# A gated layer's first block: second projection as seven products, weight differences on VectorE, last norm on ScalarE

## The chip, the cores and the metric

The kernel runs on one core of one Trainium2 chip. A core has five engines that each work through their own queue in order: TensorE (PE in the profile; its weight loads are listed apart as PEld), VectorE (DVE), ScalarE (ACT), GpSimd (POOL) and SyncE (SP, which here only issues DMAs). The metric is the device time of one execution in microseconds; the median of three runs is given. Everything is float32.

## What is computed

A transformer block on x (2 batches of 1024 tokens, 256 wide) with a context of 154 tokens, 192 wide: self attention, cross attention, and a gated layer, each with a layer norm ahead and a residual behind it. The change touches the gated layer alone:

```python
h = _layernorm(x, ln3_g, ln3_b)
p = h @ ff_w1 + ff_b1
a, gate = (p[..., :D_FF], p[..., D_FF:])
h = a * jax.nn.gelu(gate, approximate=False) @ ff_w2 + ff_b2
return h + x
```

D_FF is 1024. The first projection is 256 to 2048 wide, the second 1024 to 256.

## The kernel before

Self attention and cross attention come first (loops over p and c in the code). Behind them runs the loop of this case, over 64 *half units* k. The 2048 tokens are cut into four blocks (`pair` 0 to 3) of 512 tokens; each block has eight *units* (n, one for each 128 of the 1024 inner columns f), and a unit has two half units: `gate_first` at even k, `gate_second` at odd k. So block 0 is k 0 to 15, block 1 k 16 to 31, and so on. The order of the instructions on every engine is the order in which the code writes them: nothing is reordered. An instruction that waits holds up all that is behind it on its engine.

**The first projection** is written as a fast 2x2 matrix product: seven products (numbers 1 to 7) of 256 columns take the place of eight, out of sums and differences of the two token halves and of weights. The names: `pa`, `pb`, `pc` are PSUM banks of the unit, `own` its four rows of 256 in SBUF. In `gate_first(n)` product 1 goes to `pa`, ScalarE copies it to `own` (L1056); then `gate_last(n-1)` does product 4 of the unit before, VectorE adds (L1088), GpSimd multiplies (L1090) and so finishes that unit's first token half in `ub`; then products 6 and 5 with an addition each on VectorE (L1060, L1062) that read the copy. In `gate_second(n)` product 2 is added into `pa` (over what L1056 has read), ScalarE does a Gelu (L1074); product 7 is added into `pb` (over what L1060 has read), VectorE adds (L1076); product 3 into `pc` (over what L1062 has read), VectorE adds (L1079), ScalarE does the second Gelu (L1080), GpSimd multiplies (L1081) and finishes the second token half.

**The second projection** of a block runs beside the next block's units: `sums` holds its pieces, and each half unit takes some from the list. For blocks 1 to 3 it is again a fast product: `partial(pair, i, m)` does group m of seven for token tile i, four products of 128 columns each, with weight differences `half["t"]` (made by `column_sums`, four instructions on GpSimd at half units 18 to 26) and row sums `half["s"]` (made by `row_sums`, four instructions on GpSimd for each two units). Group 1, 6, 3 and 7 are followed by additions to x on VectorE (L1170); after groups 3 and 7 a DMA on SP's queue stores a tile of 128 tokens. For block 0 it is the plain product: 32 products of 256 columns (L1200), two in each half unit from 16 on, four additions (L1210) and four stores. The differences and row sums lie in one tile `wx`, taken by `hold_sums` at half unit 16 from a pool with two buffers (tag pT), which also holds the turned probabilities of cross attention and the weights of the gated layer.

**The norm of the second batch** (`norm_beside("ff", B - 1)`) runs beside half units 7 to 19 in steps, one at each odd half unit: a step issues, in this order, the transposes of two tiles that were normalized a step ago (L280, TensorE, stored later on ScalarE, L295), the statistics of two new tiles (L240, L241, VectorE), the deviation of two (L246, L250, GpSimd), and the normalization of two (L256 on VectorE makes the offset, then two instructions on GpSimd, L267; on ScalarE, L270, in the norms that `narrow` names). The first normalization falls to half unit 11, the last to 17.

Other work beside the loop: the end of cross attention at half units 0 to 3 (`cross_values`), four pieces of its output projection at half units 4 to 6 (L467, added to x by L474 on VectorE), `token_sums` of the next block at half units 8, 24 and 40 (L1020 to L1023, four on GpSimd), and additions of the last bias (L320, GpSimd) at each third half unit from 13 on.

Of the kernel before, what the change touches and what calls it, by code (L numbers as in the profile page):

```python
# [8 lines left out]
F32 = mybir.dt.float32  # L9
AF = mybir.ActivationFunctionType  # L10
ALU = mybir.AluOpType
AX = mybir.AxisListType

P = 128
# [4 lines left out]
def tile_transformer_block(ctx: ExitStack, tc: tile.TileContext, a: dict, out: bass.AP):  # L19
    nc = tc.nc  # L20
# [3 lines left out]
    B, S, D = x.shape  # L24
# [7 lines left out]
    NT = S // P  # L32
    GT = 4
# [17 lines left out]
    NF = DF // P  # L51
    SH = GH // 2
    TF = 2
# [5 lines left out]
    wpool = ctx.enter_context(tc.tile_pool(name="w", bufs=1))  # L59
# [13 lines left out]
    def sum_tile(name):  # L73

        return ps_o.tile([P, HB], F32, tag="po", name=name)
# [22 lines left out]
    for n in names:  # L98
        k = n_of[n]
# [67 lines left out]
    for n in names[2:]:  # L167
        own = rows[row_of[n] - n_cols:row_of[n] - n_cols + n_of[n], :]
        p = HR if n in twice else P
# [51 lines left out]
    def norm_pieces(kind, b, first=False):  # L221

        ln = {"sa": "ln1", "ca": "ln2", "ff": "ln3"}[kind]
        g0, b0 = row_of[ln + "_g"], row_of[ln + "_b"]
        st = {}
        nh = NC if kind == "ff" else NH  # L230
        order = tile_order(kind)

        def stats(t):
            if t == 0:
                st["hT"] = hT[kind, b] = p2.tile(
                    [P, nh, NC * S // nh], F32, tag="hT", name=f"hT_{ln}_{b}")
            if t % 2 == 0:
                st["mv", t] = small.tile([P, 2, 2], F32, tag="mv", name=f"mv_{ln}_{b}_{t}")
            s6 = small.tile([P, 6], F32, tag="st", name=f"st_{ln}_{b}_{t}")
            nc.vector.bn_stats(s6, xt[b, order[t] // GT][:, order[t] % GT, :])  # L240
            nc.vector.bn_aggr(st["mv", t // 2 * 2][:, t % 2, :], s6)  # L241

        def deviation(t):
            mv = st["mv", t]
            var = small.tile([P, 2], F32, tag="var", name=f"var_{ln}_{b}_{t}")
            (nc.vector if first else nc.gpsimd).tensor_scalar(  # L246
                var, mv[:, :, 1], EPS, 1.0, op0=ALU.add, op1=ALU.mult
            )
            rstd = small.tile([P, 2], F32, tag="rstd", name=f"rstd_{ln}_{b}_{t}")
            nc.gpsimd.tensor_tensor(rstd, var, power, ALU.pow)  # L250
            st["rstd", t] = rstd

        def normalize(t):
            rstd = st["rstd", t]
            off = small.tile([P, 2], F32, tag="off", name=f"off_{ln}_{b}_{t}")
            nc.vector.scalar_tensor_tensor(  # L256
                off, st["mv", t][:, :, 0], -1.0, rstd, op0=ALU.mult, op1=ALU.mult
            )
            pool, tag = (one, "xn") if narrow(kind, b) and not first else (pp_, "P")

            xn = pool.tile([P, nh, 2, D // nh], F32, tag=tag, name=f"xn_{ln}_{b}_{t}")
            st["xn", t] = xn
            for i in range(2):
                xs = xt[b, order[t + i] // GT][:, order[t + i] % GT, :]
                xs, own = xs.rearrange("p (c d) -> p c d", c=nh), xn[:, :, i, :]
                if not narrow(kind, b) or first and i == 1:
                    nc.gpsimd.tensor_scalar(  # L267
                        own, xs, rstd[:, i:i + 1], off[:, i:i + 1], op0=ALU.mult, op1=ALU.add)
                else:
                    nc.scalar.activation(  # L270
                        own, xs, AF.Identity, bias=off[:, i:i + 1], scale=rstd[:, i:i + 1])

        def turn(t):

            n = 2 if first else 1
            bank = mm_tile if first and t == 2 else spare["bank"]
            ph = [bank(f"ph_{ln}_{b}_{t}_{i}") for i in range(n)]
            for i in range(2 * D // P):

                nc.tensor.transpose(  # L280
                    ph[i * n * P // (2 * D)][:, i % (2 * D // P // n) * P:][:, :P],
                    st["xn", t].rearrange("p c i d -> p (c i d)")[:, i * P:(i + 1) * P], ident)

            def store():
                k = NC * 2 * P // nh
                for c in range(nh):
                    own = st["hT"][:, c, t // 2 * k:(t // 2 + 1) * k]
                    turned = ph[c * n // nh][:, c % (nh // n) * k:][:, :k]
                    gain, shift = cols[:, g0 + c:g0 + c + 1], cols[:, b0 + c:b0 + c + 1]
                    if spare["turned"] or first and c < nh // 2:  # L290
                        nc.vector.tensor_scalar(
                            own, turned, gain, shift, op0=ALU.mult, op1=ALU.add
                        )
                    else:
                        nc.scalar.activation(own, turned, AF.Identity, bias=shift, scale=gain)  # L295

            return store

        return (
            [lambda t=t: stats(t) for t in range(NT)],  # L300
            *([lambda t=t, f=f: f(t) for t in range(0, NT, 2)] for f in (deviation, normalize, turn)),
        )

# [6 lines left out]
    def narrow(kind, b):  # L310

        return kind == "sa" or kind == "ca" and b < B - 1
# [649 lines left out]
    NPR = B * 2  # L962
# [120 lines left out]
    def gate_last(n):  # L1083

        pair, f = divmod(n, NF)
        pa, pb, pc, own = psum.pop(n)
        product(n, 4, pb, False)
        nc.vector.scalar_tensor_tensor(  # L1088
            own[:, 0, :], pb[:, :BT], biases(n)[0], own[:, 0, :], op0=ALU.add, op1=ALU.add)
        nc.gpsimd.tensor_tensor(ub[pair][0][:, f, :], own[:, 0, :], own[:, 3, :], ALU.mult)  # L1090
        if f == NF - 1:
            if pair:
                early, late = (1, 4, 2), (5, 6, 3, 7)
                if pair == NPR - 1:
                    sums.extend((pair, i, m) for m in early for i in range(TF))
                    sums.extend((pair, i, m) for i in range(TF) for m in late)
                else:
                    sums.extend((pair, i, m) for i in range(TF) for m in early + late)
            else:
                sums.extend((pair, i, e) for i in range(2 * TF) for e in range(NF))  # L1100

    sums, summed = [], {}

# [2 lines left out]
    def hold_sums():  # L1106

        wx = pt_.tile([P, 2 * NK, QH // 2], F32, tag="pT", name="wx").rearrange("p a b -> p (a b)")
        n1, n2 = NF // 2 * P, NF // 2 * BT
        half["t"] = {  # L1110
            i: wx[:, k * n1:(k + 1) * n1].rearrange("p (c d) -> p c d", d=P)
            for k, i in enumerate((5, 6, 7, 4))
        }
        half["s"] = [
            {
                i: wx[:, 4 * n1 + (3 * e + k) * n2:][:, :n2].rearrange("p (c t) -> p c t", t=BT)
                for k, i in enumerate((5, 6, 3))
            }
            for e in range(2)
        ]  # L1120
# [4 lines left out]
    def column_sums(n):  # L1125

        t = half["t"]
        nc.gpsimd.tensor_tensor(*[
            lambda: (t[5], quarter(0, 1), quarter(0, 0)),
            lambda: (t[6], quarter(1, 1), t[5]),  # L1130
            lambda: (t[4], quarter(1, 0), t[6]),
            lambda: (t[7], quarter(1, 1), quarter(0, 1)),
        ][n](), ALU.subtract)
# [56 lines left out]

    def sum_slot():

        pair, i, f = sums.pop(0)
        if pair:
            return partial(pair, i, f)
        if f == 0:
            summed[pair] = sum_tile(f"pf{pair}_{i}")
        own = summed[pair]
        j, e = divmod(i, TF)
        nc.tensor.matmul(  # L1200
            own[:, :D], lhsT=ub[pair][j][:, f, e * P:(e + 1) * P], rhs=w2[:, f, :],
            start=(f == 0), stop=(f == NF - 1),
        )
        if f < NF - 1:
            return None
        b, t = divmod(pair * 2 * TF + i, NT)

        def store():
            xs = xt[b, t // GT][:, t % GT, :]
            nc.vector.tensor_tensor(xs, own[:, :D], xs, ALU.add)  # L1210
            nc.sync.dma_start(out=out[b, t * P:(t + 1) * P, :], in_=xs)

        return store


    with tc.manual_schedule():
# [192 lines left out]
        for k in range(2 * FU):  # L1409
# [17 lines left out]
                out_pieces("ca", B - 1, NQ - 1, out_order("ca"))  # L1427
            if k % (2 * NF) == NF and k < 2 * FU - 2 * NF:
                token_sums(k // (2 * NF) + 1)
            for _ in range(min(2 if k < 4 * NF else 1, len(sums))):  # L1430
                run(sum_slot)
            flush(stores)
            run_work(0 if k <= len(CG) else 1 + k % 2, k % 2)
            if later and k > 12 and k % 3 == 1:
                later.pop(0)()
            if k == 2 * NF:
                hold_sums()
            if k in (2 * NF + 2, 2 * NF + 4, 2 * NF + 8, 2 * NF + 10):
                column_sums((k - 2 * NF) // 3)
            pair, at = divmod(k - 5, 2 * NF)  # L1440
            if pair > 0 and at % 4 == 0:
                row_sums(pair, at // 4)
        gate_last(FU - 1)
        row_sums(NPR - 1, NF // 2 - 1)
        while sums:
# [35 lines left out]
```

## Time and profile before

| | us |
|---|---|
| median of 3 runs | 1078.59 (1078.13 to 1078.92) |
| the profiled execution, its own time | 1078.65 |
| its span, first to last instruction | 1076.9 |
| block 0 of the gated layer (half units 0 to 15) | 910.2 to 947.2 |
| half units 16 to 31 | 947.2 to 986.0 |
| half units 32 to 63 | 986.0 to 1060.4 |
| what is left of block 3 | 1060.4 to 1076.9 |

How to read it: in the order of time a row gives the start and length in us, engine, line, operation, what is written and read, and in brackets how long the engine stood idle before and who released it. `x2` behind a row means that two instructions of that form follow each other. A product in float32 appears as two matmuls. The length of a matmul is modelled and longer than the step to the next one. In a group by line the two numbers behind the bar are the busy time of all and the mean in ns of one; in the answer to a single line the three numbers are the shortest, the median and the longest in ns.

### The profile page before, as it was taken

How to read it: one execution, taken by the hardware profiler on the slowest of the kernel's cores; microseconds unless marked ns; L12 is line 12 of the kernel's file. 1: busy time of each engine (PE TensorE's matmuls, PEld its weight loads, DVE VectorE, ACT ScalarE, POOL GpSimd, SP SyncE). 2: the span in 40 equal slices, each digit the busy share in tenths (PEclk: the TensorE clock that was granted, in tenths of full speed). 3: DMA queues.
4: the chain of work that ended last, by engine and by line, in shares of the span. 5: the costliest groups of instructions: out<-in, count | busy, mean ns of one | idle time of the engine just before them, and what ended most of it. 6: DMA issues, size and time to landing. Idle time of an engine off the chain costs nothing.

```text
span 1076.9 us, 45967 instructions
## 1 busy us (share of the span) xinstructions
PE 1065.6 (99%) x19060; PEld 712.3 (66%) x19060; DVE 875.2 (81%) x1283; ACT 651.0 (60%) x2081; POOL 765.4 (71%) x1600
## 2 busy tenths in 40 slices
PE   8999999999999999999999999999999999999998
PEld 6545657567565565566665655567766677788998
DVE  5789999998989989999989998978766777654554
ACT  5666767667666666666776666666566555242221
POOL 2677777778777787777777777768665687488774
PEclk9999999999999999999999999999999999999999
DMA  3232122111111111211211211135323221000000
GB/s 95 63 91 63 46 47 46 33 43 30 41 40 33 43 43 29 53 43 24 53 24 33 53 24 38 24 103 131 97 57 83 68 58 41 1 10 11 21 11 30
DMA packets 99234, 50.56 MB, mean 47 GB/s; under 512 B 30218, under 2 KB 97810, under 8 KB 99026
## 3 DMA queue, kind: packets, MB, share of 16 engines
q1 hardware_dynamic: 97698, 46.96, 18.0%
q8 instruction: 150, 2.46, 1.0%
q10 hardware_dynamic: 1328, 0.66, 0.2%
q14 instruction: 58, 0.48, 0.1%
HBM read 35.25 MB, written 3.41 MB: 36 GB/s over the span
## 4 chain that ended last, share of the span: by engine, by line
PE 91%; POOL 3%; DVE 2%; DMA 1%; ACT 1%; issue 1%; SPq 1%; DVEq 0%; POOLq 0%; ACTq 0%
PE s L493 19%; PE po L547 19%; PE py_sa L467 5%; PE py_ca L467 5%; PE pv_sa L393 5%; PE pq_ca L362 5%; PE pq_sa L362 5%; PE pk_sa L362 5%; PE sc L867 4%; PE poc L932 4%; PE pb L1037 3%; PE pf L1161 3%; PE pa L1037 2%; PE pc L1037 2%; PE pf L1200 1%; DMA st<-st 1%
## 5 line engine op out<-in xcount | busy, mean ns | idle before, releaser
L613 POOL TENSOR_SCALAR p<-p,rd,ee 128x512 f32<-128x512 f32 x508 | 387.4, 773 | 91.4 <-DVE rd L605 88.1
L508 ACT ACTIVATE p<-s,st 128x512 f32<-128x512 f32 x512 | 345.9, 687 | 175.5 <-DVE st L502 169.7
L502 DVE TENSOR_REDUCE st<-s 128x2 f32<-128x1024 f32 x256 | 308.8, 1207 | 51.1 <-issue 20.4
L640 DVE STREAM_TRANSPOSE pT<-p 128x1024 f32<-128x1024 f32 x256 | 302.4, 1219 | 1.5 <-POOL p L613 1.5
L493 PE MATMUL s<-k_sa,q_sa 64*32 64x512 f32 x4096 | 256.1, 591 | 2.4 <-ACT p L508 1.6
L547 PE MATMUL po<-pT,v_sa 64*32 64x256 f32 x8192 | 239.5, 376 | 0.9 <-ACT p L885 0.9
L547 PEld LDWEIGHTS po<-pT,v_sa 64*32 64x32 f32 x8192 | 177.5, 106 | 71.4 <-issue 26.2
L493 PEld LDWEIGHTS s<-k_sa,q_sa 64*32 64x32 f32 x4096 | 83.5, 106 | 101.0 <-issue 52.7
L885 ACT ACTIVATE p<-sc,neg 128x154 f32<-128x154 f32 x256 | 96.9, 401 | 74.9 <-DVE rden L893 74.4
L896 POOL TENSOR_SCALAR p<-p,rden 128x154 f32<-128x154 f32 x256 | 97.4, 402 | 61.7 <-DVE rden L893 61.2
L508 ACT ACTIVATION_READ_ACCUMULATOR p<-s,st 128x1 f32 x512 | 103.4, 202 | 0.0
L526 POOL TENSOR_TENSOR dd<-st 128x8 f32<-128x8 f32 x128 | 25.9, 202 | 73.5 <-DMA st<-st 69.7
L872 DVE TENSOR_REDUCE neg<-sc 128x6 f32<-128x924 f32 (+1 forms) x48 | 48.0, 1000 | 31.0 <-PE sc L867 30.9
L393 PEld LDWEIGHTS pv_sa<-sa_wv,hT_ln 64*128 64x128 f32 x1024 | 58.5, 188 | 14.2 <-issue 9.2
L393 PE MATMUL pv_sa<-sa_wv,hT_ln 64*128 64x128 f32 x1024 | 61.7, 275 | 0.0
L467 PE MATMUL py_ca<-ca_wo,o_ca 128*128 128x256 f32 x256 | 60.8, 385 | 0.0
L467 PE MATMUL py_sa<-sa_wo,o_sa 128*128 128x256 f32 x256 | 59.8, 386 | 0.0
L467 PEld LDWEIGHTS py_sa<-sa_wo,o_sa 128*128 128x128 f32 x256 | 47.2, 190 | 18.0 <-ACT v_sa L402 5.9
L362 PE MATMUL pq_ca<-hT_ln,ca_wq 64*128 64x512 f32 (+1 forms) x352 | 58.2, 589 | 0.0
L362 PE MATMUL pk_sa<-hT_ln,sa_wk 64*32 64x512 f32 x960 | 57.1, 590 | 0.0
L362 PE MATMUL pq_sa<-hT_ln,sa_wq 64*32 64x512 f32 (+1 forms) x976 | 56.7, 586 | 0.0
L885 ACT ACTIVATION_READ_ACCUMULATOR p<-sc,neg 128x1 f32 x256 | 55.3, 216 | 0.0
(132 smaller groups left out, 1442.6 us busy)
## 6 DMA issues: line engine op xcount, KB each, us to landing
v_sa<-v_sa SPq DMA_DIRECT2D x32, 256.0 KB, 3.8
st<-st SPq DMA_DIRECT2D x510, 1.0 KB, 1.8
v_ca<-vd SPq DMA_DIRECT2D x32, 160.0 KB, 3.1
sa_wq<-in_L_xattn_sa_wq_dram SPq DMA_DIRECT2D x32, 128.0 KB, 3.2
sa_wk<-in_L_xattn_sa_wk_dram SPq DMA_DIRECT2D x32, 128.0 KB, 3.2
sa_wv<-in_L_xattn_sa_wv_dram SPq DMA_DIRECT2D x32, 128.0 KB, 3.2
ca_wq<-in_L_xattn_ca_wq_dram SPq DMA_DIRECT2D x32, 128.0 KB, 3.4
wf<-in_L_xattn_ff_w_dram SPq DMA_DIRECT2D x12, 256.0 KB, 5.3
```

The lines of the kernel that those rows point to most:

```text
L362: nc.tensor.matmul(pq[r][f:f + m, at:at + n], lhsT=wt[own, c, f:f + m], rhs=h[own, c, t0:t0 + n], start=(c == 0), stop=(c == NH - 1), tile ...
L393: nc.tensor.matmul(pv[r][:, i * P:(i + 1) * P], lhsT=h[own, c, i * P:(i + 1) * P], rhs=wt[own, c, :], start=(c == 0), stop=(c == NH - 1), ...
L467: nc.tensor.matmul(py[:, e * D:(e + 1) * D], lhsT=o[:, i, (t + e) * P:(t + e + 1) * P], rhs=wo[kind, b, g][:, i, :], start=(i == 0), stop= ...
L493: nc.tensor.matmul(sc[a4 * KB:(a4 + 1) * KB, j, :], lhsT=q[r, c:c + KB], rhs=k[r, h * HB:(h + 1) * HB], start=True, stop=True, tile_positi ...
L502: nc.vector.tensor_reduce(st[:, 0, 0, i, :], sc, AX.X, ALU.max, negate=True)
L508: nc.scalar.activation(pr[:, j, :], sc[:, j, :], AF.Exp, bias=st[:, 0, 0, i, j:j + 1], accum_out=st[:, 0, 1, i, j:j + 1],)
L547: nc.tensor.matmul(po[a2][d:d + KB, :QH // 2], lhsT=v[r, t, e, d:d + KB], rhs=pT[r, d // DH * NK + n, :], start=(t == 0 and e == 0), stop= ...
L613: nc.gpsimd.tensor_scalar(pr[:, j, :], pr[:, j, :], v["rd"][:, c:c + 1], v["ee"][:, 0, c:c + 1], op0=ALU.mult, op1=ALU.mult,)
L640: nc.vector.transpose(halves[h][:, :, c:c + KB], slot[p]["members"][i].rearrange("p j (n k) -> p (j n) k", k=KB))
L885: nc.scalar.activation(pr_[:, j, i, :T], sc[:, j, i * T:(i + 1) * T], AF.Exp, bias=neg[:, j, i:i + 1], accum_out=den[:, j, i:i + 1],)
L896: nc.gpsimd.tensor_scalar(pr_[:, j, i, :T], pr_[:, j, i, :T], rden[:, j, i:i + 1], 1.0, op0=ALU.mult, op1=ALU.mult,)
L1037: nc.tensor.matmul(into[:, :BT], lhsT=lhs, rhs=wh[pair][i], start=first, stop=True, skip_group_check=True)
```

## The change

The second projection of block 0 goes through `partial` like the others: at the end of block 0 fourteen groups are put in `sums` (for each of two token tiles: 1, 4, 2, 5, 6, 3, 7), and one is taken in each half unit from 18 on (before: two plain products from 16 on). The plain path falls away. The row sums of block 0 are made at half units 6, 10, 14 and 17; those of blocks 1 to 3 move by up to two half units. `hold_sums` comes at half unit 4; the weight differences get four tiles of their own in the buffers of attention weights that are no longer used, and `column_sums` runs on VectorE, at half units 5 to 8. The normalization of the second batch's last norm runs on ScalarE.

```diff
@@ normalize
-                if not narrow(kind, b) or first and i == 1:
+                if not narrow(kind, b) and (kind, b) != ("ff", B - 1) or first and i == 1:
                     nc.gpsimd.tensor_scalar(
                         own, xs, rstd[:, i:i + 1], off[:, i:i + 1], op0=ALU.mult, op1=ALU.add)
                 else:
...
@@ gate_last
         if f == NF - 1:
-            if pair:
-                early, late = (1, 4, 2), (5, 6, 3, 7)
-                if pair == NPR - 1:
-                    sums.extend((pair, i, m) for m in early for i in range(TF))
-                    sums.extend((pair, i, m) for i in range(TF) for m in late)
-                else:
-                    sums.extend((pair, i, m) for i in range(TF) for m in early + late)
+            early, late = (1, 4, 2), (5, 6, 3, 7)
+            if pair == NPR - 1:
+                sums.extend((pair, i, m) for m in early for i in range(TF))
+                sums.extend((pair, i, m) for i in range(TF) for m in late)
             else:
-                sums.extend((pair, i, e) for i in range(2 * TF) for e in range(NF))
+                sums.extend((pair, i, m) for i in range(TF) for m in early + late)
@@ hold_sums
-        n1, n2 = NF // 2 * P, NF // 2 * BT
+        n2 = NF // 2 * BT
         half["t"] = {
-            i: wx[:, k * n1:(k + 1) * n1].rearrange("p (c d) -> p c d", d=P)
-            for k, i in enumerate((5, 6, 7, 4))
+            i: wpool.tile([P, NF // 2, P], F32, tag=tag, name=f"w2s{i}", bufs=2 if tag == "wq" else 1)
+            for i, tag in ((5, "wq"), (6, "wq"), (7, "wk"), (4, "wv"))
         }
...
@@ column_sums
-        nc.gpsimd.tensor_tensor(*[
+        nc.vector.tensor_tensor(*[
...
@@ sum_slot
-        pair, i, f = sums.pop(0)
-        if pair:
-            return partial(pair, i, f)
...
+        return partial(*sums.pop(0))
@@ the loop over half units
-            for _ in range(min(2 if k < 4 * NF else 1, len(sums))):
+            for _ in range(min(int(k > 2 * NF + 1), len(sums))):
                 run(sum_slot)
...
-            if k == 2 * NF:
+            if k == len(CG) + 1:
                 hold_sums()
-            if k in (2 * NF + 2, 2 * NF + 4, 2 * NF + 8, 2 * NF + 10):
-                column_sums((k - 2 * NF) // 3)
+            if len(CG) + 1 < k <= NF:
+                column_sums(k - len(CG) - 2)
+            if k in (NF - 2, NF + 2, 2 * NF - 2, 2 * NF + 1):
+                row_sums(0, (k - NF + 2) // 4 + k % 2)
             pair, at = divmod(k - 5, 2 * NF)
-            if pair > 0 and at % 4 == 0:
-                row_sums(pair, at // 4)
+            ready = (2, 4, 9, 12) if pair == 1 else (0, 3, 8, 12)
+            if pair > 0 and at in ready:
+                row_sums(pair, ready.index(at))
```

More of the change, by code (lines that the diff above doesn't have):

```diff
@@ L1115, in hold_sums @@
             {
-                i: wx[:, 4 * n1 + (3 * e + k) * n2:][:, :n2].rearrange("p (c t) -> p c t", t=BT)
+                i: wx[:, (3 * e + k) * n2:][:, :n2].rearrange("p (c t) -> p c t", t=BT)
                 for k, i in enumerate((5, 6, 3))
@@ L1191, in sum_slot @@
     def sum_slot():
-        pair, i, f = sums.pop(0)
-        if pair:
-            return partial(pair, i, f)
[L1196 to L1213, printed above, removed]
+        return partial(*sums.pop(0))
     with tc.manual_schedule():
```

## The prediction

> **What bounds the kernel now.** I read the page first (busy shares, chain of waits), then a table of stages over the gated layer, then the order of time of each engine between 930 and 957 us, where the edits fall.
>
> ```profile
> span 1076.9 us, 45967 instructions
> PE 1065.6 (99%) x19060; PEld 712.3 (66%) x19060; DVE 875.2 (81%) x1283; ACT 651.0 (60%) x2081; POOL 765.4 (71%) x1600
> PE 91%; POOL 3%; DVE 2%; DMA 1%; ACT 1%; issue 1%; SPq 1%; DVEq 0%; POOLq 0%; ACTq 0%
> ```
> ```profile
> 910.20:947.20 37.00, 35.66 (x237) 28.34 (x230) 26.23 (x71) 13.35 (x30) 18.74 (x32) 1.00 0.00 1
> 947.20:986.00 38.80, 38.80 (x187) 34.18 (x186) 19.35 (x46) 13.63 (x30) 34.59 (x49) 1.00 0.03 11
> 986.00:1021.40 35.40, 35.40 (x220) 32.67 (x219) 20.28 (x47) 10.39 (x23) 26.00 (x38) 1.00 0.05 16
> ```
> The columns are stretch, length, then busy time of TensorE, its weight loads, VectorE, ScalarE and GpSimd, clock, DMA. First row: half units 0 to 15 (gated units 0 to 7 of the first block); second: half units 16 to 31, where the old second projection of that block runs; third: what follows. TensorE has no idle time from 947.2 us on. Work taken from it there is worth its full length, and a wait put on it anywhere is lost. In the first row it is not full, and its order of time shows where:
>
> ```profile
> 933.90 0.59 PE L1037 MATMUL pa<-hT_ln,wf 128*128 128x256 f32 x2
> 934.63 0.70 PE L1037 MATMUL pb<-hT_ln,wf 128*128 128x256 f32 x2
> 937.32 0.59 PE L1037 MATMUL pa<-hT_ln,wf 128*128 128x256 f32 x2
> 938.05 0.70 PE L1037 MATMUL pb<-hT_ln,wf 128*128 128x256 f32 x2
> 940.75 0.59 PE L1037 MATMUL pa<-hT_ln,wf 128*128 128x256 f32 x2
> 941.84 0.70 PE L1037 MATMUL pb<-hT_ln,wf 128*128 128x256 f32 x2 [0.49 <-DVE own L1060]
> 942.80 0.27 PE L280 MATMUL ph_ln<-ident,xn_ln 128*128 128x128 f32 x1
> 943.24 0.55 PE L280 MATMUL ph_ln<-ident,xn_ln 128*128 128x128 f32 x3 [0.16 <-POOL xn_ln L267]
> 945.35 0.59 PE L1037 MATMUL pa<-hT_ln,wf 128*128 128x256 f32 x2
> 946.64 0.86 PE L280 MATMUL ph_ln<-ident,xn_ln 128*128 128x128 f32 x4
> 947.34 0.60 PE L1037 MATMUL pa<-hT_ln,wf 128*128 128x256 f32 x2
> ```
> One product of 256 columns is two matmuls and takes 0.43 us of TensorE (945.35 to 946.64 are three). Product 7 of units 4, 5 and 6 comes 0.73, 0.73 and 1.09 after product 2, so 0.30, 0.30 and 0.66 late; the transposes are 0.33 late (0.44 after the first where 0.11 is the step), and the second set, 0.44 long, is left after 0.70 and so costs another 0.26. In all 1.85 us wait, first on VectorE, then on GpSimd's norm. So half units 8 to 15 have no cover.
>
> **The change, part by part.**
>
> *The products.* Old: 32 products of 256 columns. New: 2 token tiles x 7 groups of 4 products of 128 columns.
>
> ```profile
> 985.51 0.86 PE pf L1200 x4
> 988.10 0.89 PE pf L1161 x8
> ```
> From the chain in order of time: two old products 0.86, one new group 0.89. Old 16 x 0.86 = 13.8 us (half units 16 to 31), new 14 x 0.89 = 12.5 us (18 to 31, one a half unit: just in time before the next block's groups at 32). Term: -1.3 us, full worth. The additions to the result grow on VectorE:
>
> ```profile
> L1170 DVE TENSOR_TENSOR x<-pf,x 128x512 f32<-128x512 f32 (+2 forms) x30 | 14.2, 478 | 16.0 <-PE pf L1161 15.8
> L1210 DVE TENSOR_TENSOR x<-pf,x 128x256 f32<-128x256 f32 x4 | 1.7, 425 | 2.0 <-PE pf L1200 2.0
> ```
> 10 of the first (4.8 us) replace 4 of the second (1.7): +3.1 us in a stretch where VectorE is busy 19.35 of 38.80. Nothing; without that cover at most 3.1. The output DMAs stay four on SP's queue, at half units 23, 24, 30, 31 instead of 19, 23, 27, 31: nothing, SP carries nothing else there. Memory of the weight differences: buffers of weights long used up, no instruction. The block's sums tile is taken at half unit 4, after its old content is read at 3: nothing.
>
> *Weight differences on VectorE, half units 5 to 8.*
>
> ```profile
> L1128 POOL TENSOR_TENSOR wx<-wf 128x512 f32<-128x512 f32 x2 | 2.5, 1273 | 0.0
> 925.89 0.69 DVE L474 TENSOR_TENSOR x<-py_ca,x 128x512 f32<-128x512 f32 x1 [1.30 <-PE py_ca L467]
> 927.62 0.69 DVE L474 TENSOR_TENSOR x<-py_ca,x 128x512 f32<-128x512 f32 x1 [1.03 <-PE py_ca L467]
> ```
> Leaving GpSimd frees 5.1 us at half units 18 to 26, where nothing waits for it. No two-SBUF-operand subtraction of 512 stands on VectorE; below it lies nothing, above it GpSimd's 1.27 plus one blocked turn of 0.73 (next fence but one); I take 0.62, a little under L474's 0.69 for as many elements, one operand of it in PSUM. The first two (half units 5, 6) fall into VectorE's waits for the output projection, 1.30 and 1.03 long here. The other two meet this:
>
> ```profile
> 932.37 0.42 DVE L1079 TENSOR_TENSOR own<-pc,own 128x256 f32<-128x256 f32 x1
> 933.42 0.72 POOL L1081 TENSOR_TENSOR kT<-own 128x256 f32<-128x256 f32 x1 [3.64 <-ACT own L1080]
> 933.79 0.45 DVE L1088 SCALAR_TENSOR_TENSOR own<-pb,cols,own 128x256 f32<-128x256 f32 x1
> 934.16 0.42 DVE L1060 TENSOR_TENSOR own<-pb,own 128x256 f32<-128x256 f32 x1
> 935.36 0.48 DVE L1076 SCALAR_TENSOR_TENSOR own<-pb,cols,own 128x256 f32<-128x256 f32 x1 [0.46 <-PE pb L1037]
> 937.59 0.41 DVE L1060 TENSOR_TENSOR own<-pb,own 128x256 f32<-128x256 f32 x1
> ```
> The third enters before L1088 at 933.79, waits for L1081 to end at 934.1, takes 0.62: L1060 slips 0.9, product 7 of unit 4 with it. The fourth enters before L1076, behind L1090: VectorE's gap of 0.46 takes part of it, 0.3 more remain. Product 7 of unit 5 is then 1.2 late.
>
> That two-operand work blocks across the engines is seen at 951.77:
>
> ```profile
> 951.77 0.73 POOL L320 TENSOR_TENSOR x<-x,ff_b 128x256 f32<-128x256 f32 x1
> 951.77 0.73 DVE L256 SCALAR_TENSOR_TENSOR off_ln<-mv_ln,rstd_ln 128x2 f32<-128x2 f32 x1
> L256 DVE SCALAR_TENSOR_TENSOR off_ln<-mv_ln,rstd_ln x24: 126/161/735, 6.6 to 951.8; 128x2 f32<-128x2 f32 x24
> ```
> Two numbers a partition usually take 0.16 us; here 0.73, exactly until L320 ends. [...]
>
> *Row sums of the first block, half units 6, 10, 14, 17.*
>
> ```profile
> L1140 POOL TENSOR_TENSOR wx<-u 128x256 f32<-128x256 f32 x12 | 8.7, 729 | 0.0
> 942.09 1.10 POOL L267 TENSOR_SCALAR xn_ln<-x,rstd_ln,off_ln 128x256 f32<-128x256 f32 x2
> ```
> Four such each: 2.9 us of GpSimd, 11.7 in all, against four norms of 1.10 taken off it. The first set falls into an idle 3.6 us (row 933.42). The others pile up: GpSimd is 4 to 6 us later at half unit 18. Its gate products feed nothing that is waited for soon, and group 5, which needs the last set (I get 957.3 to 960.3), runs after 963. But the norm's reciprocal deviations queue behind them.
>
> *Last norm on ScalarE, half units 11, 13, 15, 17.*
>
> ```profile
> L270 ACT ACTIVATE xn_ln<-x,off_ln,rstd_ln x20: 586/600/607, 6.8 to 612.9; 128x256 f32<-128x256 f32 x20
> 940.10 0.35 ACT L1056 COPY own<-pa 128x256 f32<-128x256 f32 x1
> 940.64 0.41 DVE L256 SCALAR_TENSOR_TENSOR off_ln<-mv_ln,rstd_ln 128x2 f32<-128x2 f32 x1
> 944.31 0.37 ACT L1056 COPY own<-pa 128x256 f32<-128x256 f32 x1 [0.33 <-PE pa L1037]
> 944.42 0.37 DVE L256 SCALAR_TENSOR_TENSOR off_ln<-mv_ln,rstd_ln 128x2 f32<-128x2 f32 x1
> ```
> Here the loss lies. ScalarE's queue gets two norms (1.1 us) that wait for L256, and behind them stands L1056, the copy of the next unit's product 1. Product 2 overwrites what that copy reads, and L1060 reads the copy; so TensorE and VectorE both stop until it is done. Today L1056 runs before L256 is over. Walking the queues: L256 at 941.7 (1.2 late, less a shorter block), norms to 943.0, L1056 to 943.3; product 2 of unit 6 starts 943.3 (today 940.75), product 7 943.8: 1.9 late. From there L1076, L1079 and two statistics give VectorE free at 946.7; the deviation needs GpSimd, which ends L1081 of unit 5 only after the second row sums, and gives it at 946.5; L256 gets its turn by 947.2, norms to 948.4, L1056 to 948.8; product 2 of unit 7 starts 948.8 against 945.35, product 7 3.6 late at 949.2 to 949.4. The third turn (no statistics left) costs 0.5, the fourth 0.3, where today's are the 0.26 of the transposes. From half unit 18 the groups between cover it. TensorE's waits: 1.25 and 0.6 at units 4 and 5, 1.5, 2.0, 0.5, 0.3 at units 6 to 9: 6.1, in place of 1.85 now: +4.2.
>
> **Sum.** -1.3 + 4.2 = +2.9 us on the span of 1076.9, that is 1079.8; that execution took 1078.65, 0.06 over the median, so the median goes from 1078.59 to about 1081.4. After half unit 32 nothing changes: the row sums of later blocks move by one or two half units beside a full TensorE, and the tail's own are where they were.
>
> **Bounds.** A difference at no cost leaves the norm's part: +1.6. At 1.3 a piece the two uncovered ones add 1.9: +4.8. Norms of 0.45 instead of 0.55 apart: 0.2 less. No row sums ahead of the deviations: 1 less.
>
> **The rivals.**
> 1. *Only the norm costs.* VectorE finds room for the differences, as for the first two. For it: its gap of 0.46 a unit. Against: no gap between 932.37 and 934.9. -1.3 + 2.9 = +1.6: 1080.2.
> 2. *The other side: ScalarE has room and TensorE stays the bound.* If the copies come out ahead of the norms, ScalarE, busy 13.35 of 37.00, takes them free, the transposes stop waiting for GpSimd (0.33 and 0.26) and the products' -1.3 counts: -1.9, 1076.7; with all of 1.85 gone 1075.4. It decides where L256 ends before a copy's product does, 0.5 us earlier than now. Against: L256 at 940.64, L1056 at 940.10.
> 3. *Blocking multiplies.* GpSimd's row sums and VectorE's differences and L256 shut each other out in turn, each difference takes 1.3, and the deviations come later: +4.8, 1083.4. For it: the 0.73. Against: L256 is held for one instruction only.
>
> **How the numbers follow.** Forecast 0.50, rival 1 0.20, rival 2 0.12, rival 3 0.18. About 0.2% (2.2 us) is what can be told from no change: slower means above 1080.75. The forecast with its own spread of 1080.2 to 1082.6 lies above in four fifths of its cases (0.40), rival 3 all (0.18), rival 1 a little (0.03): slower 0.61. Faster, below 1076.4, is half of rival 2: 0.06. Same 0.33. Range 1078.0 to 1083.8: it leaves out most of rival 2 and the top of rival 3.
>
> **What would show it.** In the changed profile: L1170 x40 and no L1200; TensorE full from half unit 18 on; L1056 of units 6 to 9 starting as the norm's second activation ends; product 2 waiting for ScalarE there, 4 us in all; VectorE's differences 0.6 to 0.7 when alone. Wrong if the copies run ahead of the norms, if product 7 of unit 5 is not about 1 us late, or if a group between half units 19 and 31 waits for GpSimd.

## The result, and the profile after

| | before | changed |
|---|---|---|
| median of 9 runs, us | 1078.46 (1077.61 to 1079.63) | 1081.41 (1080.77 to 1083.19) |
| profiled execution, its own time | 1078.65 | 1081.6 |
| its span | 1076.9 | 1079.8 |
| first product of half unit 0 to first product of half unit 32 ("the stretch") | 75.99 | 78.45 |

The changed kernel is slower: ratio 1.0029, 95% interval 1.002 to 1.0038. By the medians that is 2.95 us, by the interval between 2.2 and 4.1. The forecast was 1081.4.

The busy shares on the page of the changed kernel:

```profile
PE 1065.2 (99%) x19108; PEld 710.8 (66%) x19108; DVE 879.9 (81%) x1293; ACT 654.4 (61%) x2089; POOL 765.3 (71%) x1604
```

TensorE is busy 0.4 us less than before (1065.2 against 1065.6) and the span is 2.9 longer: what was added is waiting, not work.

Now the table of stages, laid from product to product so that both kernels are cut at the same instruction. First the kernel before, half units 0 to 15 and 16 to 31:

```profile
910.22:947.34 37.12, 35.78 (x238) 28.48 (x231) 26.37 (x71) 13.38 (x31) 18.88 (x32) 1.00 0.00 1
947.34:986.21 38.87, 38.87 (x186) 34.23 (x185) 19.21 (x45) 13.80 (x31) 34.66 (x49) 1.00 0.03 11
```

Then the changed kernel, the same two parts:

```profile
910.73:950.92 40.19, 35.80 (x239) 28.39 (x231) 28.91 (x74) 15.28 (x34) 24.49 (x38) 1.00 0.00 1
950.92:989.18 38.26, 38.13 (x234) 34.44 (x233) 21.77 (x52) 15.44 (x35) 31.59 (x47) 1.00 0.03 9
```

The stretch is 2.46 us longer with 0.7 less of TensorE's busy time in it. The loss lies in the first part, which is 3.07 longer: TensorE is idle 4.39 us there, 1.34 before. The second part is 0.61 shorter. It holds the products' gain of 1.3, and 0.7 of that is lost again in small delays at units 8 and 9. What follows the stretch is the same length in both (1076.9 - 986.21 = 90.7, 1079.8 - 989.18 = 90.6). The remaining 0.5 us of the span is older than the gated layer: its first product comes at 910.73 instead of 910.22, behind code that is the same in both. In the twelve traces of this study that first product falls between 909.41 and 912.29, so a single span can be off by a microsecond or two for reasons that have nothing to do with the edits. From here on kernels are compared by the stretch, and the medians stand beside it. The stretch is read from one execution of each kernel, but it repeats well: half units 0 to 7, which no edit lengthens, take 21.95 or 21.96 us in all twelve traces, and what follows half unit 32 takes 90.6 or 90.7.

The changed kernel's TensorE in order of time, each late product with the row ahead of it:

```profile
934.41 0.59 PE L1037 MATMUL pa<-hT_ln,wf 128*128 128x256 f32 x2
935.98 0.70 PE L1037 MATMUL pb<-hT_ln,wf 128*128 128x256 f32 x2 [0.98 <-DVE own L1060]
...
938.80 0.59 PE L1037 MATMUL pa<-hT_ln,wf 128*128 128x256 f32 x2
939.51 0.70 PE L1037 MATMUL pb<-hT_ln,wf 128*128 128x256 f32 x2
...
941.77 0.59 PE L1037 MATMUL pc<-hs,w1s 128*128 128x256 f32 x2
943.72 0.70 PE L1037 MATMUL pa<-hT_ln,wf 128*128 128x256 f32 x2 [1.35 <-ACT own L1056]
...
946.88 0.59 PE L1037 MATMUL pc<-hs,w1s 128*128 128x256 f32 x2
949.05 0.70 PE L1037 MATMUL pa<-hT_ln,wf 128*128 128x256 f32 x2 [1.58 <-ACT own L1056]
...
952.22 0.59 PE L1037 MATMUL pc<-hs,w1s 128*128 128x256 f32 x2
952.94 0.70 PE L1037 MATMUL pa<-hT_ln,wf 128*128 128x256 f32 x2
...
956.60 1.05 PE L1158 MATMUL pf<-wf,u 128*128 128x128 f32 x8
957.58 0.70 PE L1037 MATMUL pa<-hT_ln,wf 128*128 128x256 f32 x2
```

From each pair the step of 0.43 (0.89 behind the group of the last pair) is taken off. That leaves 1.14 at product 7 of unit 4, 0.28 at product 7 of unit 5, 1.52 at product 2 of unit 6, 1.74 at product 2 of unit 7, 0.29 at unit 8 and 0.09 at unit 9: 5.1 us, and with the lags of about 0.1 behind late products (0.53 or 0.54 to the next product, as from 935.98 to 936.52, instead of 0.43), as far as the kernel before doesn't have them too, some 5.6. The stretch says the same: 75.99 less the old waits of 1.85 less the products' 1.3 is 72.84, and 78.45 is 5.6 over that.

ScalarE of the changed kernel, in order of time, the two turns that cost most:

```profile
942.32 1.09 ACT L270 ACTIVATE xn_ln<-x,off_ln,rstd_ln 128x256 f32<-128x256 f32 x2 [0.68 <-DVE off_ln L256]
943.32 0.35 ACT L1056 COPY own<-pa 128x256 f32<-128x256 f32 x1
...
947.66 1.09 ACT L270 ACTIVATE xn_ln<-x,off_ln,rstd_ln 128x256 f32<-128x256 f32 x2 [1.34 <-DVE off_ln L256]
948.65 0.35 ACT L1056 COPY own<-pa 128x256 f32<-128x256 f32 x1
```

The copy that TensorE waits for starts in the moment the second normalization is over, and the normalizations start when L256 lets them: ScalarE itself had been idle for 0.68 and 1.34 us. Who holds L256 up is read from the chain of waits of the changed kernel, in order of time (start, length, engine, what):

```profile
942.14 0.69 POOL wx L1137
...
944.43 0.68 POOL kT L1140
945.12 0.69 POOL kT L1081
...
946.15 0.71 POOL rstd_ln L250
946.89 0.68 DVE off_ln L256
947.66 1.09 ACT xn_ln L270 x2
948.75 0.27 ACT own L1056
949.05 0.70 PE pa L1037 x2
```

The chain runs through GpSimd: the second set of row sums, then the multiply L1081, then the deviation L250, then VectorE's L256, and last ScalarE and TensorE. Two orders of issue thus lie on the path, row sums ahead of the deviation and norms ahead of the copy.

### The profile page after: what moved, and what is told of

Same layout as the page of the kernel before. It is cut to its first block, busy times and chain, and to the rows that moved or that the text cites. A ratio compares the mean times of both kernels' runs of the same rounds, so it can differ in the third digit from the quotient of the medians.

```text
span 1079.8 us, 46101 instructions
## 1 busy us (share of the span) xinstructions
PE 1065.2 (99%) x19108; PEld 710.8 (66%) x19108; DVE 879.9 (81%) x1293; ACT 654.4 (61%) x2089; POOL 765.3 (71%) x1604
## 4 chain that ended last, share of the span: by engine, by line
PE 88%; POOL 3%; DVE 3%; ACT 2%; DMA 2%; issue 1%; SPq 1%; DVEq 0%; POOLq 0%; ACTq 0%
PE s L493 19%; PE po L547 19%; PE py_sa L467 5%; PE py_ca L467 5%; PE pv_sa L393 5%; PE pq_sa L362 5%; PE pk_sa L362 5%; PE pq_ca L362 4%; PE pf L1158 4%; PE sc L867 4%; PE poc L932 4%; PE pb L1037 3%; PE pa L1037 2%; PE pc L1037 2%; DMA st<-st 1%; ACT p L508 1%
```

## The experiments

Theory: three edits put waits on TensorE in half units 8 to 17, where it has no cover. These are the third and fourth weight difference on VectorE, the norms ahead of the copy on ScalarE, and the row sums ahead of the deviations on GpSimd; only the order in the queues matters. The rivals are those of the prediction: the norm alone costs; the engines have room; blocking between VectorE and GpSimd is the main price. Ten kernels were run. Length of the stretch (by the table of stages, cut as above), median and ratio to the kernel before:

| kernel | stretch | against 75.99 | median, us | before, same chip | ratio, 95% interval |
|---|---|---|---|---|---|
| changed | 78.45 | +2.46 | 1081.41 | 1078.46 | 1.0029, 1.002 to 1.0038 |
| 1 changed, copies ahead of norms | 77.29 | +1.30 | 1080.29 | 1079.07 | 1.0014, 1.0004 to 1.0023 |
| 2 changed, differences early | 77.19 | +1.20 | 1081.04 | 1079.07 | 1.002, 1.001 to 1.0029 |
| 3 changed, row sums late | 77.80 | +1.81 | 1082.32 | 1079.07 | 1.0028, 1.0015 to 1.0041 |
| 4 changed, norm back on GpSimd | 82.40 | +6.41 | 1085.33 | 1079.07 | 1.0061, 1.0046 to 1.0076 |
| 5 before, norm on ScalarE | 77.98 | +1.99 | 1081.14 | 1079.12 | 1.0022, 1.0012 to 1.0031 |
| 6 before, norm on ScalarE behind the copy | 76.10 | +0.11 | 1079.44 | 1079.12 | 1.0003, 0.9994 to 1.0012 |
| 7 before, differences on VectorE | 77.07 | +1.08 | 1080.56 | 1079.12 | 1.001, 1.0001 to 1.002 |
| 8 changed, 1 + 2 + 3 together | 74.85 | -1.14 | 1078.32 | 1079.12 | 0.9993, 0.9984 to 1.0001 |
| 9 changed, norm eight half units later | 73.90 | -2.09 | 1076.39 | 1078.36 | 0.998, 0.9972 to 0.9989 |
| 10 as 9, and differences early | 73.27 | -2.72 | 1075.51 | 1078.36 | 0.9971, 0.9961 to 0.9982 |

In each row the difference of the stretches lies within what the interval allows for the medians.

### 1. Copies ahead of the norms

The norms' instructions on ScalarE are put aside and issued one half unit later, behind that half unit's L1056 (seven lines are added, so L1056 is L1063 here, L1060 is L1067, L256 is L257).

```diff
+    behind = []
...
-                    nc.scalar.activation(
-                        own, xs, AF.Identity, bias=off[:, i:i + 1], scale=rstd[:, i:i + 1])
+                    def scaled(own=own, xs=xs, i=i):
+                        nc.scalar.activation(
+                            own, xs, AF.Identity, bias=off[:, i:i + 1], scale=rstd[:, i:i + 1])
+
+                    if (kind, b) == ("ff", B - 1):
+                        behind.append(scaled)
+                    else:
+                        scaled()
...
             (gate_second if k % 2 else gate_first)(k // 2)
+            flush(behind)
```

> Changed kernel, with the last norm's two ScalarE instructions issued one half unit later, behind the next unit's copy L1056. Measure: the stretch from the first product of half unit 0 to the first of half unit 32, 78.45 us in the changed kernel and 75.99 before. Queue theory (the copies stand behind the norms): product 2 of units 6 to 8 no longer waits for ScalarE (now 1.52, 1.74, 0.29); what is left is waits on VectorE's L1060, with the row sums' backlog still ahead of the offset L256; stretch about 77.4 (-1.1). Rival, GpSimd's backlog alone: L256 is as late as before and all behind it on VectorE too, so less than 0.3 is gained. Rival, the products: no change.

Measured: 77.29, a gain of 1.16. No wait for the copy is left in this kernel. The wait at unit 7 is not gone, it has moved: TensorE, then VectorE of this kernel:

```profile
947.93 0.70 PE L1044 MATMUL pb<-hT_ln,wf 128*128 128x256 f32 x2 [1.63 <-DVE own L1067]
```
```profile
946.48 0.67 DVE L257 SCALAR_TENSOR_TENSOR off_ln<-mv_ln,rstd_ln 128x2 f32<-128x2 f32 x1 [1.23 <-POOL rstd_ln L251]
...
947.47 0.41 DVE L1067 TENSOR_TENSOR own<-pb,own 128x256 f32<-128x256 f32 x1
```

VectorE's queue has the same fault as ScalarE's: the offset waits 1.23 us for GpSimd's deviation, and the addition that product 7 needs stands behind it. So the order on ScalarE was the price at unit 6. At unit 7, with that order mended, GpSimd's lateness still is.

### 2. Differences early

All four differences are issued at half units 5 and 6, where VectorE waits for the output projection.

```diff
-            if len(CG) + 1 < k <= NF:
-                column_sums(k - len(CG) - 2)
+            if k in (len(CG) + 2, len(CG) + 3):
+                column_sums(2 * (k - len(CG) - 2))
+                column_sums(2 * (k - len(CG) - 2) + 1)
```

> Changed kernel, with all four weight differences on VectorE at half units 5 and 6 (two each) and none at 7 and 8. Queue theory: product 7 of unit 4 waits about 0.4 in place of 1.14, unit 5 about 0.3, the rest as it is; stretch from half unit 0 to 32 about 77.4 (78.45 in the changed kernel, -1.1). Rival, the differences are hidden or blocked alike wherever they stand: no more than 0.2 either way. Rival, the norm alone: no change.

Measured: 77.19, a gain of 1.26. What TensorE waits for between 910 and 960 us in this kernel (total, times, longest):

```profile
PE pa L1037 <- ACT own L1056: 2.6, 2, 1.6
PE pb L1037 <- DVE own L1076: 0.4, 1, 0.4
```

The wait for L1060 at unit 4 is gone and the waits for the copy stay. The differences thus have a price of their own, which speaks against "only the norm costs".

### 3. Row sums late

```diff
-            if k in (NF - 2, NF + 2, 2 * NF - 2, 2 * NF + 1):
-                row_sums(0, (k - NF + 2) // 4 + k % 2)
+            if k in (NF - 2, 2 * NF - 1, 2 * NF + 1, 2 * NF + 2):
+                row_sums(0, (NF - 2, 2 * NF - 1, 2 * NF + 1, 2 * NF + 2).index(k))
```

> Changed kernel, with the first block's second to fourth row sums at half units 15, 17 and 18 in place of 10, 14 and 17. Queue theory: the deviations come earlier, L256 of the second turn no longer waits for GpSimd, product 2 of unit 7 waits 1.2 to 1.4 in place of 1.74, those of units 8 and 9 next to nothing; stretch from half unit 0 to 32 about 77.4 to 77.9 (78.45 in the changed kernel). Rival, GpSimd's backlog is the whole cause: all of the waits for ScalarE go, stretch about 75 (-3.5). Rival, the backlog costs nothing: 78.4.

Measured: 77.80, a gain of 0.65. The waits for the copy fall from 2.9 to 2.5 us in total. The median is no better than the changed kernel's; it is from five runs with an interval of 1.6 to 4.4 us over the kernel before, so it neither shows nor excludes a gain of this size. In this execution the gated layer began at 912.29, the latest of all.

### 4. The norm back on GpSimd

```diff
-                if not narrow(kind, b) and (kind, b) != ("ff", B - 1) or first and i == 1:
+                if not narrow(kind, b) or first and i == 1:
```

> Changed kernel, with the last norm's two instructions on GpSimd again. Queue theory: no wait for ScalarE is left, but the norm stands behind the row sums on GpSimd and the transposes wait for it, about 4 us at the first and 3.7 at the third; stretch from half unit 0 to 32 about 82.3 (78.45 in the changed kernel, +3.9). Rival, the norm on ScalarE is the loss and taking it back mends it: stretch about 75.5 to 76.5. Rival, GpSimd has room: about 77.

Measured: 82.40, 3.95 more than the changed kernel. So the move to ScalarE isn't the fault by itself: with the row sums on GpSimd, leaving the norm there is worse. The number agrees with the expectation by offset. The waits for the norm were smaller than reckoned: 5.2 us over three in the view of waits and 5.8 by the steps from product to product (3.49, 1.85 and 0.42), where about 7.7 had been expected. Something else was lost. TensorE of this kernel, then its table of stages:

```profile
948.52 1.44 PE L280 MATMUL ph_ln<-ident,xn_ln 128*128 128x128 f32 x4 [3.33 <-POOL xn_ln L267]
949.76 1.06 PE L1037 MATMUL pa<-hT_ln,wf 128*128 128x256 f32 x2
...
952.15 0.59 PE L1037 MATMUL pc<-hs,w1s 128*128 128x256 f32 x2
...
953.88 0.60 PE L280 MATMUL ph_ln<-ident,xn_ln 128*128 128x128 f32 x4
...
955.61 0.59 PE L1037 MATMUL pc<-hs,w1s 128*128 128x256 f32 x2
```
```profile
948.50:952.10 3.60, 3.51 (x10) 2.77 (x11) 0.39 (x1) 1.19 (x3) 3.44 (x7) 0.53 0.00 0
```

Behind 3.33 us of idle time the four transposes and three products from 948.52 to 952.15 take 3.63 us, at a granted clock of 0.53. The same work takes 1.73 from 953.88 to 955.61. So 1.9 us came on top of the wait. The changed kernel's 78.45, less the 3.6 of its waits for the copy, plus 5.8 and 1.9, is 82.5; measured 82.40.

### 5 and 6. The norm alone, on the kernel before

Number 5 is the one line of `normalize` in the change, on the kernel before. Number 6 adds to it the edit of number 1.

```diff
-                if not narrow(kind, b) or first and i == 1:
+                if not narrow(kind, b) and (kind, b) != ("ff", B - 1) or first and i == 1:
```

> Kernel before, with one part of the change alone: the last norm on ScalarE. Queue theory: the copies of units 6 and 7 stand behind the norms, product 2 waits 1.9 and 1.4, the waits of the transposes go; stretch from half unit 0 to 32 about 77.9 (75.99 before, +1.9). Rival, ScalarE has room (busy 13.35 of 37.00): the transposes' 0.6 is won, 75.4. Rival, the loss needs the row sums' backlog: 76.0.

> Kernel before, with the last norm on ScalarE, but its instructions one half unit later, behind the next copy L1056. Queue theory: no wait of product 2 for ScalarE is left, the transposes find their operands; stretch from half unit 0 to 32 about 75.7 (75.99 before, -0.3). Rival, the norm costs on ScalarE wherever it stands: 77.9.

Measured: 77.98 and 76.10. TensorE in number 5:

```profile
941.75 0.70 PE L1037 MATMUL pa<-hT_ln,wf 128*128 128x256 f32 x2 [1.64 <-ACT own L1056]
...
946.66 0.70 PE L1037 MATMUL pa<-hT_ln,wf 128*128 128x256 f32 x2 [1.15 <-ACT own L1056]
```

With no row sums and no differences moved, the copy is late all the same: by the steps the two waits are 1.81 and 1.32 (1.9 and 1.4 were expected). Behind the copy, the same instructions on the same engine cost 0.11 in the stretch, which is no difference. The 1.99 is the price of the place in the queue and not of ScalarE's time. Nor is it a gain, where 0.3 had been expected: TensorE's wait of 0.2 for GpSimd's norm (in the view of waits) gives way to one of 0.2 for the stores of the transposes on ScalarE (L302), now behind the norms.

### 7. The differences alone, on the kernel before

`hold_sums` at half unit 4 with tiles of their own, differences on VectorE at half units 5 to 8, nothing else.

```diff
...
-        nc.gpsimd.tensor_tensor(*[
+        nc.vector.tensor_tensor(*[
...
-            if k == 2 * NF:
+            if k == len(CG) + 1:
                 hold_sums()
-            if k in (2 * NF + 2, 2 * NF + 4, 2 * NF + 8, 2 * NF + 10):
-                column_sums((k - 2 * NF) // 3)
+            if len(CG) + 1 < k <= NF:
+                column_sums(k - len(CG) - 2)
```

> Kernel before, with the weight differences alone moved: on VectorE at half units 5 to 8, in tiles of their own. Queue theory: product 7 of unit 4 waits 1.1 to 1.3 in place of 0.30, the norm on GpSimd then comes later and the transposes with it; stretch from half unit 0 to 32 about 77.4 (75.99 before, +1.4). Rival, VectorE has room: 76.0.

Measured: 77.07. The wait at unit 4 is the changed kernel's to the hundredth (0.98 by the bracket), with the norm still on GpSimd and no row sums of block 0:

```profile
936.55 0.70 PE L1037 MATMUL pb<-hT_ln,wf 128*128 128x256 f32 x2 [0.98 <-DVE own L1060]
```

Numbers 5 and 7 and the gain of number 3 now close the sum: 1.99 + 1.08 + 0.65 - 1.3 = +2.4 against 2.46 measured. That it closes so well is partly luck, since the parts aren't independent: within the change, mending the norm's order gains 1.16 and not 1.99 (number 1).

### 8. All three orders mended

Edits 1, 2 and 3 in one kernel.

> Changed kernel with all three orders mended: norms behind the copies, all differences at half units 5 and 6, row sums at half units 6, 15, 17, 18. Queue theory: what is left of the waits in half units 7 to 19 is about 2.3 us on VectorE's statistics, against 5.5 in the changed kernel and 1.85 before, and the products' gain of 1.3 counts; stretch from half unit 0 to 32 about 74.5 to 75 (75.99 before), time about 1077.5 against 1078.5 before and 1081.4 changed. Rival, the products (seven of 128 columns cost more than they save): no faster than before, 76 or more.

Measured: 74.85; against the changed kernel 3.60 less, more than the three gains one by one (1.16 + 1.26 + 0.65 = 3.07): where two queues hold the same product up, mending one alone uncovers the other. The median is 0.8 us under the kernel before, and the interval reaches to 1.0001, so the time can't be told from no change.

### 9 and 10. The norm later

The last norm's steps begin at half unit 15 instead of 7, so its four normalizations fall to half units 19 to 25, where a group of the second projection (0.89) stands in every half unit. Number 10 adds edit 2.

```diff
-            if k == 2 * len(CG) + 1:
+            if k == 2 * NF - 1:
                 norm_beside("ff", B - 1)
```

> Changed kernel, with the last norm's steps begun at half unit 15 in place of 7, so that its normalizations fall to half units 19 to 25, where a group of four products (0.89 us) stands between one unit's product 5 and its product 2. Queue theory: nothing is reordered within a step, but the copy behind the norms has time, and VectorE's statistics lie in a stretch where it is half idle; the waits of units 6 to 9 for ScalarE go, product 7 of unit 4 waits about 0.4; stretch from half unit 0 to 32 about 73.5 to 74 (75.99 before, 78.45 changed). Rival, the norm on ScalarE or the statistics cost the same wherever they stand: 77 to 78.5. Rival, the next block's token sums at half unit 24, which need the norm's first four tiles, now wait for it and block GpSimd: 75 to 77.

> As norm_later, and all four weight differences on VectorE at half units 5 and 6. Queue theory: some 0.4 us less wait than norm_later, stretch about 73.2 to 73.8, time about 1076 against 1078.5 to 1079.1 before: faster than both kernels. Rival, with the statistics gone from half units 7 and 8 the place of the differences makes no difference: the same as norm_later.

Measured: 73.90 and 73.27. Number 10 is faster than both kernels of this case: 0.9971 of the kernel before (0.9961 to 0.9982), 1075.51 us. ScalarE, and then TensorE, at one of its turns:

```profile
954.64 1.09 ACT L270 ACTIVATE xn_ln<-x,off_ln,rstd_ln 128x256 f32<-128x256 f32 x2 [1.02 <-DVE off_ln L256]
955.64 0.35 ACT L1056 COPY own<-pa 128x256 f32<-128x256 f32 x1
```
```profile
954.64 0.59 PE L1037 MATMUL pc<-hs,w1s 128*128 128x256 f32 x2
955.07 1.05 PE L1158 MATMUL pf<-wf,u 128*128 128x128 f32 x8
956.04 0.70 PE L1037 MATMUL pa<-hT_ln,wf 128*128 128x256 f32 x2
```

The bad order is unchanged: the copy still starts as the norms end, and ScalarE waited 1.02 us for L256. But TensorE has a group of 0.89 to do in that time, and product 2 comes 0.97 behind it: 0.08 late instead of 1.5, and behind the three other turns it isn't late. The one other delay of note is at 947.56, 0.40 behind its turn. 72.84 + 0.48 is 73.32; measured 73.27. Not all of this gain is ScalarE's: the norm's statistics on VectorE moved along, out of the half units without cover, and in number 10 the old waits of 1.85 went with them.

## Why the prediction was right, step by step

*The products, -1.3.* Right. They weren't run without the other edits, but the traces show the term between the first products of half units 22 and 32, where TensorE waits in neither kernel. Where that begins, before and then changed:

```profile
962.47 0.59 PE L1037 MATMUL pa<-hT_ln,wf 128*128 128x256 f32 x2
```
```profile
965.14 0.60 PE L1037 MATMUL pa<-hT_ln,wf 128*128 128x256 f32 x2
```

To the stretch's ends at 986.21 and 989.18 these are 23.74 and 24.04. So each of the ten groups takes 0.03 longer than the two products in its place, 0.4 for fourteen, and the two half units that have none save 0.86 each: -1.3. The sum of number 10 (73.32 against 73.27) needs the same term.

*The additions on VectorE, cost nothing.* Right. The group of additions in the changed kernel:

```profile
L1167 DVE TENSOR_TENSOR x<-pf,x 128x512 f32<-128x512 f32 (+2 forms) x40 | 18.9, 477 | 19.5 <-PE pf L1158 19.2
```

There are 40, as forecast, and nearly all idle time ahead of them is VectorE waiting for TensorE; from 956 to 990 us the view of waits has none for TensorE, so neither these additions nor the output's DMAs nor group 5 held it up.

*Weight differences.* Right that they make product 7 late, and nearly right in size. VectorE of the changed kernel:

```profile
925.02 0.68 DVE L1125 TENSOR_TENSOR w2s<-wf 128x512 f32<-128x512 f32 x1
...
930.23 0.69 DVE L1125 TENSOR_TENSOR w2s<-wf,w2s 128x512 f32<-128x512 f32 x1
...
934.31 0.89 DVE L1125 TENSOR_TENSOR w2s<-wf,w2s 128x512 f32<-128x512 f32 x1
...
936.18 0.77 DVE L1125 TENSOR_TENSOR w2s<-wf 128x512 f32<-128x512 f32 x1
```

One costs 0.68, not the 0.62 that was taken; the third started 0.35 before the end of L1081 (933.93 to 934.66) and took 0.89, 0.2 longer, where a wait of 0.3 for that end was reckoned. No run shows the 0.3 itself. Units 4 and 5 waited 1.14 and 0.28 where 1.25 and 0.6 were forecast: VectorE made up more of the fourth than was reckoned. The part as a whole was put at 1.3 (the sum without it was to be +1.6); it measured 1.08 alone and 1.26 within the change.

*Last norm on ScalarE, "here the loss lies".* Right. The copy stands behind two norms that wait, and product 2 of unit 6 came at 943.72 and of unit 7 at 949.05, against 943.3 and 948.8 on an axis that began 0.5 earlier. Waits of 1.52 and 1.74 were measured for 1.5 and 2.0. The third and fourth turn cost 0.29 and 0.09 for 0.5 and 0.3.

*Row sums.* Right that they reach TensorE only through the deviation; the forecast said "1 less" without them ahead of the deviations, and moving them back gave 0.65. What the prediction told under the norm, that the deviation of the second turn comes late through GpSimd, weighs more than its wording suggests: after number 1 it still held product 7 of unit 7 back, which waited 1.63 us, and with the row sums late as well (number 8) that wait is gone.

*The sum.* The waits were put at 6.1 and came to 5.6; so the stretch grew by 2.46 and not 2.9. That the span nonetheless came out at 1079.8 to the tenth is chance: the missing 0.5 arose ahead of the gated layer. The median's 2.95 has an interval that holds both. One bound doesn't follow from its terms: at 1.3 a piece instead of 0.62 two differences add 1.4 and not 1.9, so +4.3 where +4.8 stands. Rival 3's 1083.4 rests on it too.

*The signs.* Product 2's delays at units 6 to 9 are 3.6 us in all where 4 was forecast. Product 7 of unit 5 comes at 939.51, which is 0.95 later than before (938.05, on an axis 0.51 earlier), where about 1 was the sign and 1.2 the working. No copy ran ahead of its norms, and no group waited for GpSimd.

*The rivals.* "Only the norm costs" falls with numbers 2 and 7: the differences have a price of their own. "ScalarE has room" was true of the engine (15.28 busy of 40.19) and false of its queue; numbers 5 and 6 are the same work in two places, 1.88 apart. "Blocking multiplies" falls with the lengths above: 0.89 and 0.77 on the path, not 1.3. Its 1.26 does occur elsewhere (below), where VectorE had time.

## What to carry to other kernels

Here an instruction that waits was priced by what stood behind it in its queue, not by its length: the same norms cost 1.99 us ahead of the copy and 0.11 behind it, on an engine that was idle more than half of the time (busy 30.83 of 77.98 us in number 5, 30.91 of 76.10 in number 6). Before work is moved to an idle engine, list the short instruction that the bound engine needs next and see on which side of the newcomer it lands; then do the same on the engines that the newcomer itself waits for, since mending one queue of two uncovered the other (the wait of 1.63 us for VectorE in number 1). Where the order can't be changed, move the work to where the bound engine has something of its own to do: a group of 0.89 us in each half unit made the same bad order all but free, product 2 being 0.08 late instead of 1.5. With the statistics moved along, that turned +2.46 into -2.09, and with the differences early into -2.72.

## What the runs showed of the hardware that was not expected

*GpSimd was slower beside VectorE too.* The prediction reckoned with a VectorE instruction held up by GpSimd. In the changed kernel two instructions of GpSimd took longer as well, each beside one of VectorE's weight differences:

```profile
930.25 1.26 POOL L1137 TENSOR_TENSOR wx<-kT 128x256 f32<-128x256 f32 x1
...
936.36 1.17 POOL L1020 TENSOR_TENSOR hs<-hT_ln 128x256 f32<-128x256 f32 x1
```

The three other executions of each took 0.72 or 0.73. VectorE's differences started at 930.23 and 936.18, before them, and ran 0.69 and 0.77, where one alone took 0.68: in these two pairs the one that started first kept its time, or nearly, and the other took 0.53 and 0.44 longer. In number 10 it went the other way. GpSimd, then VectorE:

```profile
925.87 0.72 POOL L1081 TENSOR_TENSOR kT<-own 128x256 f32<-128x256 f32 x1 [3.64 <-ACT own L1080]
```
```profile
925.16 0.68 DVE L1125 TENSOR_TENSOR w2s<-wf 128x512 f32<-128x512 f32 x1
925.88 1.26 DVE L1125 TENSOR_TENSOR w2s<-wf,w2s 128x512 f32<-128x512 f32 x1
```

The second difference started 0.01 behind L1081 and took 1.26, 0.58 more than the first; L1081 kept its 0.72.

*The clock was lower behind a long wait.* In number 4, 3.33 us of idle time on TensorE were followed by 3.6 us (948.50 to 952.10) at a granted clock of 0.53, and the 3.9 us behind these by one of 1.00. The waits of up to 1.6 us in the changed kernel left it at 1.00 (941.50 to 945.50 and 946.90 to 951.00).
